# Gated window attention on one core: part of the output products, a gate and the sums of the last group rearranged

## The chip, the cores and the metric

The kernel runs on one core of a Trainium2 chip. The metric is the device time of one execution, in microseconds (us), taken as the median of the runs. All times below are in us unless ns is said.

## The reference

Eight batches of 1024 tokens with 512 features are normalised, sent through an attention with 16 heads of 32 features, multiplied by a gate, and added to the input. The mask repeats every 256 tokens: token i sees token j where i mod 256 is not below j mod 256.

```python
xn = _layernorm(x, axis=-1)
# attention, per head:
scores = jnp.einsum('bhid,bhjd->bhij', q, k) / jnp.sqrt(dk)
im = jnp.arange(L) % W                       # W = 256
scores = jnp.where(im[:, None] >= im[None, :], scores, NEG_INF)
attn = jnp.einsum('bhij,bhjd->bhid', softmax(scores), v)
s = jnp.einsum('bld,ed->ble', attn_as_rows, Wo) + bo
# gate:
w = (weights >= 0.0) * 2.0 - 1.0
g = _silu(jnp.clip(jnp.einsum('bsi,oi->bso', xn, w) * scale + bias, -100, 100))
x = x + s * g
```

q, k and v are products of xn with Wq, Wk and Wv plus their biases.

## The kernel before

A batch has 8 tiles of 128 tokens. Tokens are put in an order in which the mask is nearly triangular, so that much of the score matrix is never computed. The 16 heads are taken in four groups of four (NC = 4); a step of the program's main loop (line 1109) works on one group of one batch, and on one of nine *quads* (NQ = 9). A quad is a block of scores of four heads, 128 keys by 512 queries in all, and fills the one PSUM tile "quad" of four banks. There are 8 x 4 x 9 such steps.

In step n of group (b, g), `probs_quad` (586) computes the scores of the quad (the shift by the maximum, the mask and the product of keys and queries are matmuls into the same PSUM) and one exp of 128 x 2048 on ScalarE. The result goes into a tile "p" of two buffers, or, for quads 0 and 7, into the tile "total" of its half. `attend_quad` (633) multiplies the quad before with the values. Every group has two halves f of 512 queries: f = 1 has quads 0 to 6, f = 0 has quads 6 to 8 (quad 6 belongs to both). Beside this, `maxima_quad` (501) computes the same scores of the *next* group in the same PSUM tile and VectorE takes their maxima. The last group of all has no next one, and so no maxima.

The softmax's denominators: in all groups but the last, GpSimd adds the quads up in the tile "total" (`add_probs`, 649), and one product with ones per half sums over the keys (`sum_keys`, 678). In the last group `sum_quad` (693) sums every quad with its own product on TensorE. `keep_sum` (673) copies sums out of PSUM on ScalarE, `invert` (713) takes reciprocals on VectorE, one part of 128 queries at a time, and `normalise_heads` (717) multiplies with the attention of the half (PSUM tile "av", two buffers).

All other matmuls are `product`s (346): four chunks of four matmuls into one tile "bank" of PSUM (a pool of two), and an `after` that empties it. Such are queries and keys (`heads_work`), values (`values_work`), the plain gates, and the outputs (`output_work`, 726: product with Wo over the four groups, then on VectorE the bias bo is added and the gate multiplied, and GpSimd adds the residual). A gate (`gate_work`, 417) is either one in two passes of 8 fast matmuls ("G" in the plans) or a plain product of 16 matmuls ("H"). Its `after` scales and shifts on VectorE (both read the PSUM tile) and clamps on GpSimd; then `squash` (tanh on ScalarE), `finish` (VectorE) and a store to DRAM follow as pieces of work of their own. An output tile fetches its gate tile from there.

The order of the work is written out by hand. Each group has a plan, a string of words (lines 804 to 821): "q20" is half 0 of the queries of group 2, "V4" the values of tile 4, "O4" output tile 4 of the batch before, "G2" and "H2" the gate of tile 2, a ' means the next batch; words ahead of a bar may be run in the group before already. Squash and finish of a gate in the last batch are put three and four words behind it. `Beside.fill` (953) runs this work beside the steps: the costs of a group's words are spread evenly over its nine steps, and chunks are split to fit. [...]

The last group of batch 7 has the plan "-", no work of its own. After it come the eight output tiles of batch 7, in the order 4, 5, 6, 7, 0, 1, 2, 3, with tiles fetched two ahead; the inversion of each tile of half 0 is put one tile ahead (1207 to 1224). The last tile goes out in two halves, on SyncE's and ScalarE's queues (`last_output`, 750). Stores and fetches of all other tiles stand on SyncE's queue in program order.

Of the kernel before, what the change touches and what calls it, by code (L numbers as in the profile page):

```python
# [9 lines left out]
F32 = mybir.dt.float32  # L10
# [63 lines left out]
def tile_gated_window_attention(  # L74
# [554 lines left out]

    av = {}  # L630
    aT = {}

    def attend_quad(b, g, n):
        segs, _ = segments(n)
# [53 lines left out]
            )  # L688
        keep_sum(b, g, f, ps)

    sums = {}

    def sum_quad(b, g, n):

        segs, _ = segments(n)
        for k, (f, j, lo, w, at) in enumerate(segs):
            first = n == FIRST[f]
            last = n == LAST[f] and all(s[0] != f for s in segs[k + 1 :])
            if first:
                sums[f] = bank(f"sum_{b}_{g}_{f}")  # L700
            for h in range(NH):
                nc.tensor.matmul(  # L702
                    sums[f][head_rows(h), lo : lo + w],
                    lhsT=ones,
                    rhs=pts[b, g, n][:, h, at : at + w],
                    start=first,
                    stop=last,
                    skip_group_check=True,
                )
            if last:  # L710
                keep_sum(b, g, f, sums[f])

    def invert(b, g, f, part):
        r = aT[b, g, f][:, part * P : (part + 1) * P]
# [2 lines left out]
    def normalise_heads(b, g, f, part=None):  # L717
        cols = slice(0, HALF) if part is None else slice(part * P, (part + 1) * P)
        nc.vector.tensor_tensor(  # L719
            aT[b, g, f][:, cols], av[b, g, f][:, cols], aT[b, g, f][:, cols], ALU.mult  # L720
        )


    back = {}

    def output_work(b, it):
        def fetch():
            g = xres.tile([P, D], F32, tag="io", name=f"gb_{b}_{it}")
            nc.sync.dma_start(g, gd[b][it])

            where, tag = (xres, "io") if b + 1 < B else (xpool, "x")
            xr = where.tile([P, D], F32, tag=tag, name=f"xb_{b}_{it}")
            nc.sync.dma_start(xr, tokens(x, b, it))
            back[it] = g, xr

        def after(ps):
            gb, xr = back.pop(it)
            s = temp(f"s_{b}_{it}")
            nc.vector.tensor_tensor(ps, ps, rows["bo"], ALU.add)
            nc.vector.tensor_tensor(s, ps, gb, ALU.mult)  # L740
            nc.gpsimd.tensor_tensor(s, s, xr, ALU.add)  # L741
            nc.sync.dma_start(tokens(out, b, it), s)

        pairs = [
            (lambda g=g: (aT[b, g, it // 4][:, (it % 4) * P : (it % 4 + 1) * P], wT["wo"][:, g, :]))
            for g in range(NC)
        ]
        return fetch, product(f"o_ps_{b}_{it}", pairs, 0.86, after, lambda: it in back, True)

    def last_output(b, it):  # L750

        gb, xr = back.pop(it)
        s = temp(f"s_{b}_{it}")

        def ahead():
            nc.gpsimd.tensor_tensor(s, gb, rows["bo"], ALU.mult)
            nc.gpsimd.tensor_tensor(xr, xr, s, ALU.add)  # L757

        def rest():
            for part, queue in enumerate((nc.sync, nc.scalar)):  # L760
                at = slice(part * 256, part * 256 + 256)
                ps = bank(f"o_ps_{b}_{it}_{part}")
                for g in range(NC):
                    for h in range(NH):
                        cols = slice((it % 4) * P + h * DK, (it % 4) * P + (h + 1) * DK)
                        nc.tensor.matmul(
                            ps[head_rows(h), 0:256],
                            lhsT=aT[b, g, it // 4][:, cols],
                            rhs=wT["wo"][:, g, at],
                            start=(g == 0),  # L770
                            stop=(g == NC - 1),
                            skip_group_check=True,
                        )
                nc.vector.tensor_tensor(s[:, at], ps[:, 0:256], gb[:, at], ALU.mult)  # L774
                nc.vector.tensor_tensor(s[:, at], s[:, at], xr[:, at], ALU.add)  # L775
                queue.dma_start(tokens(out, b, it)[:, :, at], s[:, at])

        return ahead, rest

    def row_work():  # L780
# [20 lines left out]

    STEADY = (
# [10 lines left out]
    )  # L815
    CLOSING = (
# [4 lines left out]
    )  # L821

    class Block:
        def __init__(self, at, main):
# [17 lines left out]
    def plan(b, g, text):  # L842
        for word in text.split():
            kind, number = word[0], word.strip("'")[1:]
            bb = b + word.count("'")
            i = len(blocks)
            if kind == "|":
                for block in blocks:
                    block.early = block.early or block.at == (b, g)
                continue  # L850
            if kind == "N":
                half = int(number)
                stats, scale, normalise, turn = norm_work(b + 1, half)
                for k in range(4):
                    done = lambda key=(b + 1, 4 * half + k): key in normed
                    there = lambda key=(b + 1, 4 * half + k): key in xt
                    link(
                        i - 5 + (2 + k // 2 if half else 0) + k // 2,
                        Work(0, stats[k], late=True, ready=there),
                    )  # L860
                    by = lambda key=(b + 1, half): key in scaled
                    link(i + half + max(1, k), Work(0, normalise[k], ready=by))
                    link(i + half + 2 + k, Work(0.5, turn[k], turn=True, ready=done))
                link(i - 2 + 2 * half, Work(0, scale, late=True, ready=there))
                continue
            if kind == "-":
                main = []
            elif kind in "qk":
                main = heads_work(bb, int(number[0]), int(number[1]), kind)
            elif kind == "V":  # L870
                main = values_work(bb, int(number))
            elif kind == "W":
                main = [Work(0.5, turn_weight("wo")[int(number)], turn=True)]
            elif kind == "R":
                spread, main = row_work()
                link(i - 3, spread)
            elif kind == "O":
                fetch, main = output_work(b - 1, int(number))
                link(i - 1, fetch)
            else:  # L880
                split, main, squash, finish = gate_work(bb, int(number), kind == "H")
                if split is not None:
                    link(i - 3, split)
                later = 1 if b in (0, B - 1) else 0
                link(i + 2 + later, squash)
                link(i + 3 + later, finish)
            blocks.append(Block((b, g), main))

    for b in range(B):
        for g in range(NC):  # L890
            n0 = len(blocks)
            plan(b, g, (OPENING if b == 0 else STEADY if b + 1 < B else CLOSING)[g])
            if b + 1 == B:
                continue
            if g == 0:
                for it in range(4):
                    link(n0 + 1 + it, lambda b=b, it=it: load_x(b + 1, it))
            elif g == 1:
                for k in range(4):

                    ready = lambda key=(b + 1, k - 1): key[1] < 0 or key in turned
                    fn = lambda b=b, it=4 + k: load_x(b + 1, it)
                    link(n0 + 5 + k, Work(0, fn, ready=ready), True)
# [205 lines left out]
    for s, (b, g, n) in enumerate(steps):  # L1109
# [22 lines left out]
        probs_quad(b, g, n)  # L1132
        if s:
            attend_quad(*steps[s - 1])
            if last and n:
                sum_quad(*steps[s - 1])
            else:
                add_probs(*steps[s - 1], held=True)
        if add:
            sum_keys(*add)  # L1140
            invert(*add, 0)
# [14 lines left out]
        if nxt is not None:  # L1156
# [2 lines left out]
                shift_parts(1)  # L1159
            if n == 8:  # L1160
                shift_parts(0)
        if not last:

            add_probs(b, g, n)
        if add:
# [36 lines left out]

    b, g = B - 1, NC - 1
    attend_quad(b, g, NQ - 1)
    sum_quad(b, g, NQ - 1)
    units = {it: output_work(b, it) for it in range(NT)}
    order = (4, 5, 6, 7, 0, 1, 2, 3)
    for it in order[:2]:
        units[it][0]()
    for i, it in enumerate(order):  # L1210
        if i + 2 < NT:
            units[order[i + 2]][0]()
        if i + 1 < NT and order[i + 1] < 4:

            invert(b, g, 0, order[i + 1])
# [1 line left out]
        if it == order[-1]:  # L1217
            rest()
            continue
        if it == order[-2]:  # L1220
            ahead, rest = last_output(b, order[-1])
            ahead()
        for w in units[it][1]:
            w.run()
# [45 lines left out]
```

## Time and profile before

| | us |
|---|---|
| median of 3 runs | 2217.09 (2216.05 to 2217.92) |
| the profiled execution's own time | 2218.44 |
| its span | 2216.6 |
| last group, first scores to end of the last sum | 2148.63 to 2183.15 |
| eight output tiles and the last stores | 2183.15 to 2216.6 |

Sizes of operations (mean of one, ns): exp of 128x2048 on ScalarE 1878; reciprocal of 128x128 on VectorE 928; addition of 128x512 on GpSimd in `add_probs` 1284, for the residual 1369; VectorE operations of 128x512 with an operand in PSUM 691. The granted TensorE clock is 1.00 in the last group and 0.97 behind it. 256 KB fetches of the gate land after 2.9 (median), of the residual's input after 3.1, stores after 2.5; the two last stores of 128 KB after 2.3 and 2.9.

The busy times by stretch give, for each stretch of the span, its length and the busy time of each engine. In the timeline, each line is: start, length, engine, line of the program, operation, output and inputs, count, and in brackets the idle time of the engine before it with what ended it. In the chain of waits each line is a start, a length and the work or wait that the end of the program hung on.

### The profile page before, as it was taken

To read this page: it belongs to the slowest core of one execution; us is meant where nothing else is said; L and a number is where in the kernel's file an instruction comes from. 1 tells how busy PE (TensorE), PEld (TensorE's weight loads), DVE (VectorE), ACT (ScalarE), POOL (GpSimd) and SP (SyncE) were. 2 spreads that over 40 slices of the span, in tenths; PEclk is the share of its full clock that TensorE was granted. 3 is DMA by queue.
4 is the path that set the end of the run, shared out by engine and by line. 5 is a ranking of instruction groups with operands and counts; after the bars stand their busy time and mean duration, and the time that the engine had idled before them with its cause. 6 is when DMAs were issued, how large, how long until landed. Compare 5 with 4: busy or idle time off the path is not lost. (4 is left out here: it accounts for less than half of the span.)

```text
span 2216.6 us, 57362 instructions
## 1 busy us (share of the span) xinstructions
PE 2185.2 (99%) x26015; PEld 857.7 (39%) x26015; DVE 1276.9 (58%) x1635; ACT 875.2 (39%) x862; POOL 1325.5 (60%) x1198
## 2 busy tenths in 40 slices
PE   8999999999999999999999999999999999999998
PEld 4334333343333443333333333334333443333333
DVE  4556556665557655566555665565655665555564
ACT  2235433443444444344343443434443443343332
POOL 1256566656566656576557665556765666755662
PEclk9999999999999999999999999999999999999999
DMA  4001000121001210012000120002200111000113
GB/s 167 2 16 32 13 7 30 54 73 35 25 26 39 72 35 25 25 57 74 16 25 25 63 68 16 25 25 68 63 16 26 44 63 59 11 20 25 44 54 125
DMA packets 49676, 93.60 MB, mean 42 GB/s; under 512 B 5388, under 2 KB 5656, under 8 KB 49432
## 3 DMA queue, kind: packets, MB, share of 16 engines
q1 hardware_dynamic: 48728, 88.76, 12.2%
q8 instruction: 203, 3.33, 0.6%
q10 hardware_dynamic: 704, 1.18, 0.2%
q14 instruction: 41, 0.34, 0.0%
HBM read 56.37 MB, written 33.55 MB: 41 GB/s over the span
## 5 line engine op out<-in xcount | busy, mean ns | idle before, releaser
L659 POOL TENSOR_TENSOR p<-p,p 128x512 f32<-128x512 f32 x930 | 1096.3, 1209 | 394.2 <-ACT p L627 240.6
L537 DVE TENSOR_REDUCE pm<-s 128x4 f32<-128x2048 f32 (+3 forms) x384 | 663.8, 1749 | 589.9 <-PE s L525 588.1
L627 ACT ACTIVATE p<-t 128x2048 f32<-128x2048 f32 x288 | 540.8, 1878 | 843.9 <-PE t L614 769.4
L715 DVE RECIPROCAL aT<-aT 128x128 f32<-128x128 f32 x256 | 230.3, 928 | 217.6 <-ACT aT L676 217.6
L525 PE MATMUL s<-k,q 32*128 32x512 f32 (+3 forms) x3072 | 315.3, 504 | 1.6 <-ACT q L401 0.8
L640 PE MATMUL av<-p,v 128*32 128x512 f32 (+3 forms) x3072 | 308.2, 496 | 1.9 <-DVE aT L719 1.4
L614 PE MATMUL t<-q,k 32*128 32x512 f32 (+3 forms) x3072 | 306.7, 493 | 0.0
L358 PE MATMUL k_ps<-xnT,wkT 128*32 128x512 f32 (+3 forms) x2824 | 254.9, 478 | 1.7 <-ACT wkT L274 0.7
L358 PE MATMUL q_ps<-xnT,wqT 128*32 128x512 f32 (+2 forms) x2656 | 254.5, 497 | 2.0 <-ACT xnT L329 1.0
L358 PE MATMUL v_ps<-wvT,xnT 128*32 128x512 f32 (+3 forms) x2720 | 254.7, 490 | 0.0
L358 PE MATMUL o_ps<-woT,aT 128*32 128x512 f32 (+2 forms) x2584 | 244.1, 501 | 1.5 <-ACT shift L572 0.8
L741 POOL TENSOR_TENSOR s<-s,xb 128x512 f32<-128x512 f32 x63 | 86.2, 1369 | 216.5 <-DVE s L740 214.4
L614 PEld LDWEIGHTS t<-q,k 32*128 32x128 f32 x3072 | 139.1, 185 | 25.8
L358 PEld LDWEIGHTS k_ps<-xnT,wkT 128*32 128x32 f32 x2824 | 83.3, 109 | 168.9 <-issue 138.9
L640 PEld LDWEIGHTS av<-p,v 128*32 128x32 f32 x3072 | 70.5, 108 | 197.0 <-issue 164.4
L358 PEld LDWEIGHTS q_ps<-xnT,wqT 128*32 128x32 f32 x2656 | 78.7, 109 | 174.5 <-issue 151.8
L358 PEld LDWEIGHTS v_ps<-wvT,xnT 128*32 128x32 f32 x2720 | 78.9, 109 | 168.2 <-issue 143.5
L525 PEld LDWEIGHTS s<-k,q 32*128 32x128 f32 x3072 | 116.9, 184 | 53.5 <-ACT p L627 43.7
L456 PE MATMUL y_ps<-fwT,x 128*128 128x512 f32 x464 | 135.3, 418 | 1.7 <-ACT k L401 1.3
L358 PEld LDWEIGHTS o_ps<-woT,aT 128*32 128x32 f32 x2584 | 76.7, 110 | 152.8 <-issue 134.7
L429 POOL TENSOR_TENSOR x<-xnT,x 128x512 fp32r<-128x512 f32 x58 | 74.1, 1278 | 101.1 <-ACT x L428 101.1
L435 POOL TENSOR_SCALAR y<-y 128x512 f32<-128x512 f32 x64 | 39.6, 619 | 153.9 <-DVE y L434 111.8
(96 smaller groups left out, 1476.7 us busy)
## 6 DMA issues: line engine op xcount, KB each, us to landing
g<-t SPq DMA_DIRECT2D x64, 256.0 KB, 2.0
gb<-g SPq DMA_DIRECT2D x64, 256.0 KB, 2.9
xb<-in_L_attn_x_dram SPq DMA_DIRECT2D x64, 256.0 KB, 3.1
out_dram<-s SPq DMA_DIRECT2D x63, 256.0 KB, 2.5
x<-in_L_attn_x_dram SPq DMA_DIRECT2D x62, 256.0 KB, 3.1
wq_st<-in_L_attn_Wq_dram SPq DMA_DIRECT2D x2, 512.0 KB, 6.4
wv_st<-in_L_attn_Wv_dram SPq DMA_DIRECT2D x2, 512.0 KB
fw_st<-in_L_ffn_weights_dram SPq DMA_DIRECT2D x2, 512.0 KB, 9.4
```

What stands on the lines that cost most here:

```text
L358: nc.tensor.matmul(hold[0][cols, lo:hi], lhsT=lhsT[:, cols], rhs=rhs[:, lo:hi], start=(i == 0 and lo == 0), stop=(i == n - 1), skip_group_ ...
L429: nc.gpsimd.tensor_tensor(part[1], src, part[0].bitcast(F32), ALU.subtract)
L435: nc.gpsimd.tensor_scalar(y[0], y[0], MAX_VAL, -MAX_VAL, ALU.min, ALU.max)
L456: nc.tensor.matmul(hold[0], lhsT=part[i][:, c, :], rhs=wT["fw"][:, c, :], start=(i == 0 and c == 0), stop=(i == 1 and c == NC - 1),)
L525: nc.tensor.matmul(sc[:, h, at : at + w], lhsT=qt[b, g][head_rows(h), i * P : (i + 1) * P], rhs=kt[b, g][head_rows(h), lo:hi], start=(at = ...
L537: nc.vector.tensor_reduce(pm[:, 0 if lo == 0 else 1, i, :], sc[:, :, at : at + w], AX.X, ALU.max)
L614: nc.tensor.matmul(sc[:, h, at : at + w], lhsT=kt[b, g][head_rows(h), j * P : (j + 1) * P], rhs=qt[b, g][head_rows(h), q0 : q0 + w], start ...
L627: nc.scalar.activation(pt[:, :, :width], sc[:, :, :width], AF.Exp, scale=SCALE)
L640: nc.tensor.matmul(av[b, g, f][head_rows(h), lo : lo + w], lhsT=vt[b, j][:, g * P + h * DK : g * P + (h + 1) * DK], rhs=pts[b, g, n][:, h, ...
L659: nc.gpsimd.tensor_tensor(t[:, hs, lo : lo + w], t[:, hs, lo : lo + w], p[:, hs, at : at + w], ALU.add)
L715: nc.vector.reciprocal(r, r)
L741: nc.gpsimd.tensor_tensor(s, s, xr, ALU.add)
```

## The change

1. The last but one batch has a plan of its own for its last group, BEFORE_LAST, without G1'. The gate of tile 1 becomes the plain gate H1 in the last group.
2. In the last group, after H1, three of the four chunks (groups 0 to 2 of the heads) of output tiles 4, 5, 6, 0 and 1 are run beside the exps ("P4 P5 P6 P0 P1", `first_output`). Their `after` adds bo and keeps the partial sum in SBUF. They are ready once the half of group 2 that they read is normalised (`ended`).
3. GpSimd adds up quads 1 to 5 of half 1, and quad 6 of half 0, as in the other groups; `sum_last` makes one product over the total and one over the quad that is left. `sum_quad` goes.
4. Behind the last group the tiles go in the order 4, 7, 5, 2, 6, 3, 0, 1. Those begun have one chunk left, and add the partial sum where others add bo. Tiles are fetched three ahead, the gate tiles into the pool of the values. The last tile (now 1, begun) multiplies by the gate inside PSUM and adds the prepared residual from there; its preparation is issued ahead of tile 3, not of the last but one tile.

```diff
+    def sum_last(b, g, f, n):
+        ps = bank(f"sum_{b}_{g}_{f}")
+        own = [(lo, w, at) for f2, j, lo, w, at in segments(n)[0] if f2 == f]
+        parts_of = [(pts[b, g, TOTAL[f]], 0, HALF, 0)] + [(pts[b, g, n], *seg) for seg in own]
+        for k, (p, lo, w, at) in enumerate(parts_of):
             for h in range(NH):
                 nc.tensor.matmul(
+                    ps[head_rows(h), lo : lo + w],
                     lhsT=ones,
+                    rhs=p[:, h, at : at + w],
...
+        keep_sum(b, g, f, ps)
...
+    def first_output(b, it):
+        def after(ps):
+            n = len(begun)
+            if n % 2 == 0:
+                two[0] = qk.tile([P, L], F32, tag="qk"[n // 2 % 2], name=f"begun_{it}")
+            begun[it] = two[0][:, n % 2 * D : (n % 2 + 1) * D]
+            nc.vector.tensor_tensor(begun[it], ps, rows["bo"], ALU.add)
+        return product(
+            f"o_ps_{b}_{it}_begun", [(lambda g=g: output_pair(b, it, g)) for g in range(NC - 1)],
+            0.86, after, lambda: (b, NC - 2, it // 4) in ended, True,
+        )
...
-            g = xres.tile([P, D], F32, tag="io", name=f"gb_{b}_{it}")
+            where, tag = (xres, "io") if b + 1 < B else (vpool, "v")
+            g = where.tile([P, D], F32, tag=tag, name=f"gb_{b}_{it}")
...
-            nc.vector.tensor_tensor(ps, ps, rows["bo"], ALU.add)
+            nc.vector.tensor_tensor(ps, ps, rows["bo"] if row is None else row, ALU.add)
...
-                nc.vector.tensor_tensor(s[:, at], ps[:, 0:256], gb[:, at], ALU.mult)
-                nc.vector.tensor_tensor(s[:, at], s[:, at], xr[:, at], ALU.add)
+                nc.vector.tensor_tensor(ps[:, 0:256], ps[:, 0:256], gb[:, at], ALU.mult)
+                nc.vector.tensor_tensor(s[:, at], ps[:, 0:256], xr[:, at], ALU.add)
...
+    BEFORE_LAST = STEADY[:3] + ("k01' V1' | q11' G0' V2' k10' V3' k11' q10'",)
     CLOSING = (
         "V4 V5 | q20 V7 V6 k20 q21 k21",
         "O4 O5 | q30 k30 O6 q31 O7 k31",
         "H2 O0 H3 O1 H4 O2 H5 O3 H6 H7 |",
-        "-",
+        "H1 P4 P5 P6 P0 P1",
     )
...
-            if last and n:
-                sum_quad(*steps[s - 1])
-            else:
-                add_probs(*steps[s - 1], held=True)
+            add_probs(*steps[s - 1], held=True)
+            if last and n == LAST[1] + 1:
+                sum_last(b, g, 1, n - 1)
...
-        if not last:
+        if not last or n < LAST[1]:
             add_probs(b, g, n)
...
-    sum_quad(b, g, NQ - 1)
-    units = {it: output_work(b, it) for it in range(NT)}
-    order = (4, 5, 6, 7, 0, 1, 2, 3)
-    for it in order[:2]:
+    sum_last(b, g, 0, NQ - 1)
+    order = (4, 7, 5, 2, 6, 3, 0, 1)
+    units = {it: output_work(b, it, begun.get(it)) for it in range(NT)}
+    for it in order[:3]:
         units[it][0]()
     for i, it in enumerate(order):
-        if i + 2 < NT:
-            units[order[i + 2]][0]()
+        if i + 3 < NT:
+            units[order[i + 3]][0]()
...
-        if it == order[-2]:
-            ahead, rest = last_output(b, order[-1])
+        if it == order[-3]:
+            ahead, rest = last_output(b, order[-1], begun[order[-1]])
             ahead()
```

More of the change, by code (lines that the diff above doesn't have):

```diff
@@ L631, in tile_gated_window_attention @@
     aT = {}
+    ended = set()
     def attend_quad(b, g, n):
@@ L689, in sum_keys @@
         keep_sum(b, g, f, ps)
[L691 to L700, printed above, removed]
+    def sum_last(b, g, f, n):
[3 more added lines that the diff above has]
+        for k, (p, lo, w, at) in enumerate(parts_of):
             for h in range(NH):
                 nc.tensor.matmul(
-                    sums[f][head_rows(h), lo : lo + w],
+                    ps[head_rows(h), lo : lo + w],
                     lhsT=ones,
-                    rhs=pts[b, g, n][:, h, at : at + w],
-                    start=first,
-                    stop=last,
+                    rhs=p[:, h, at : at + w],
+                    start=(k == 0),
+                    stop=(k == len(own)),
                     skip_group_check=True,
                 )
-            if last:
-                keep_sum(b, g, f, sums[f])
+        keep_sum(b, g, f, ps)
     def invert(b, g, f, part):
@@ L721, in normalise_heads, with output_pair, output_work @@
         )
+        ended.add((b, g, f))
     back = {}
-    def output_work(b, it):
+    begun, two = {}, {}
+    def output_pair(b, it, g):
+        return (
+            aT[b, g, it // 4][:, (it % 4) * P : (it % 4 + 1) * P], wT["wo"][:, g, :]
+        )
[9 more added lines that the diff above has]
+            0.86, after, lambda: (b, NC - 2, it // 4) in ended, True,
+        )
+    def output_work(b, it, row=None):
         def fetch():
-            g = xres.tile([P, D], F32, tag="io", name=f"gb_{b}_{it}")
+            where, tag = (xres, "io") if b + 1 < B else (vpool, "v")
+            g = where.tile([P, D], F32, tag=tag, name=f"gb_{b}_{it}")
             nc.sync.dma_start(g, gd[b][it])
@@ L744, in output_work, with last_output @@
         pairs = [
-            (lambda g=g: (aT[b, g, it // 4][:, (it % 4) * P : (it % 4 + 1) * P], wT["wo"][:, g, :]))
-            for g in range(NC)
+            (lambda g=g: output_pair(b, it, g))
+            for g in range(0 if row is None else NC - 1, NC)
         ]
         return fetch, product(f"o_ps_{b}_{it}", pairs, 0.86, after, lambda: it in back, True)
-    def last_output(b, it):
+    def last_output(b, it, row):
         gb, xr = back.pop(it)
@@ L755, in ahead @@
         def ahead():
-            nc.gpsimd.tensor_tensor(s, gb, rows["bo"], ALU.mult)
+            nc.gpsimd.tensor_tensor(s, gb, row, ALU.mult)
             nc.gpsimd.tensor_tensor(xr, xr, s, ALU.add)
@@ L762, in rest @@
                 ps = bank(f"o_ps_{b}_{it}_{part}")
[L763 to L773, printed above, removed]
-                nc.vector.tensor_tensor(s[:, at], ps[:, 0:256], gb[:, at], ALU.mult)
-                nc.vector.tensor_tensor(s[:, at], s[:, at], xr[:, at], ALU.add)
+                lhsT, rhs = output_pair(b, it, NC - 1)
+                for h in range(NH):
+                    nc.tensor.matmul(
+                        ps[head_rows(h), 0:256], lhsT=lhsT[:, head_rows(h)], rhs=rhs[:, at],
+                        start=True, stop=True, skip_group_check=True,
+                    )
+                nc.vector.tensor_tensor(ps[:, 0:256], ps[:, 0:256], gb[:, at], ALU.mult)
+                nc.vector.tensor_tensor(s[:, at], ps[:, 0:256], xr[:, at], ALU.add)
                 queue.dma_start(tokens(out, b, it)[:, :, at], s[:, at])
@@ L819, in tile_gated_window_attention @@
         "H2 O0 H3 O1 H4 O2 H5 O3 H6 H7 |",
[1 row of a table removed]
[1 row of a table added]
     )
+    BEGUN = (4, 5, 6, 0, 1)
     class Block:
@@ L865, in plan @@
                 continue
-            if kind == "-":
-                main = []
-            elif kind in "qk":
+            if kind in "qk":
                 main = heads_work(bb, int(number[0]), int(number[1]), kind)
@@ L871, in plan @@
                 main = values_work(bb, int(number))
+            elif kind == "P":
+                main = first_output(bb, int(number))
             elif kind == "W":
@@ L887, in plan @@
             blocks.append(Block((b, g), main))
+    PLANS = [OPENING] + [STEADY] * (B - 3) + [BEFORE_LAST, CLOSING]
     for b in range(B):
@@ L891, in tile_gated_window_attention @@
             n0 = len(blocks)
-            plan(b, g, (OPENING if b == 0 else STEADY if b + 1 < B else CLOSING)[g])
+            plan(b, g, PLANS[b][g])
             if b + 1 == B:
@@ L1204, in tile_gated_window_attention @@
     attend_quad(b, g, NQ - 1)
-    sum_quad(b, g, NQ - 1)
-    units = {it: output_work(b, it) for it in range(NT)}
-    order = (4, 5, 6, 7, 0, 1, 2, 3)
-    for it in order[:2]:
+    sum_last(b, g, 0, NQ - 1)
+    order = (4, 7, 5, 2, 6, 3, 0, 1)
+    assert set(begun) == set(BEGUN)
+    units = {it: output_work(b, it, begun.get(it)) for it in range(NT)}
+    for it in order[:3]:
         units[it][0]()
     for i, it in enumerate(order):
-        if i + 2 < NT:
-            units[order[i + 2]][0]()
+        if i + 3 < NT:
+            units[order[i + 3]][0]()
         if i + 1 < NT and order[i + 1] < 4:
```

## The prediction

> **What bounds it now.** I read the page first, then the busy times by stretch (for the whole span and for the last two stages), then the chain that ended last, then TensorE, VectorE, GpSimd and SyncE in order of time for the last two groups.
>
> ```profile
> PE 2185.2 (99%) x26015; PEld 857.7 (39%) x26015; DVE 1276.9 (58%) x1635; ACT 875.2 (39%) x862; POOL 1325.5 (60%) x1198
> ...
> 2148.60:2183.20 34.60, 30.92 (x412) 12.49 (x416) 15.50 (x26) 19.47 (x14) 3.63 (x4) 1.00 0.21 70
> 2183.20:2216.60 33.40, 27.61 (x288) 9.19 (x280) 16.53 (x26) 0.58 (x1) 11.44 (x9) 0.97 0.43 143
> ```
>
> TensorE is busy 99% of the span. The second and third lines are the stages the change is about (length, then busy PE, weight loads, DVE, ACT, POOL): the last group, and the eight output tiles after it. GpSimd does 3.63 us of work in the first and is free.
>
> ```profile
> 2170.60 0.40 PE t L592 x8
> 2171.00 0.11 PE t L603 x8
> 2171.11 0.96 PE t L614 x16
> ...
> 2172.16 1.89 ACT p L627
> 2174.04 0.04 issue
> 2174.09 0.40 PE t L592 x4
> ...
> 2183.15 9.83 PE o_ps L358 x89
> ...
> 2203.87 3.58 DMA gb<-g
> ```
>
> In the last group the chain alternates: scores, exp (1.89), scores. There is one score quad in PSUM, so a step takes 3.33 to 3.49. Beside the exp PE does attention (0.88) and the sum (0.86); some 0.4 a step is lost. From 2183.15 eight products of 3.43 follow, and 33.45 pass to the end. Call the first scores of the group t(0), 2148.63, and the end of its last sum T0, 2183.15: 34.5 lie between.
>
> ```profile
> 2087.58 0.41 PE L566 MATMUL mT_ps<-identb,mt 128*32 128x128 bf16 x16 [0.26 <-DVE y L434]
> 2094.83 4.96 POOL L659 TENSOR_TENSOR p<-p,p 128x512 f32<-128x512 f32 x4
> 2099.82 0.61 POOL L435 TENSOR_SCALAR y<-y 128x512 f32<-128x512 f32 x1
> 2101.80 4.96 POOL L659 TENSOR_TENSOR p<-p,p 128x512 f32<-128x512 f32 x4 [1.37 <-ACT p L627]
> 2107.59 1.66 POOL L741 TENSOR_TENSOR s<-s,xb 128x512 f32<-128x512 f32 x1 [0.83 <-DVE s L740]
> 2123.18 5.23 POOL L659 TENSOR_TENSOR p<-p,p 128x384 f32<-128x384 f32 x5
> 2194.86 0.94 DVE L715 RECIPROCAL aT<-aT 128x128 f32<-128x128 f32 x1
> 2195.83 0.29 DVE L719 TENSOR_TENSOR aT<-av,aT 128x128 f32<-128x128 f32 x1
> 2196.95 0.70 DVE L739 TENSOR_TENSOR o_ps<-o_ps,bo_r 128x512 f32<-128x512 f32 x1 [0.83 <-PE o_ps L358]
> 2197.68 0.69 DVE L740 TENSOR_TENSOR s<-o_ps,gb 128x512 f32<-128x512 f32 x1
> ```
>
> These price what comes: adding one quad on GpSimd costs 4.96 (5.23 for the split one), the gate's clamp 0.61. The first line is a product that waits until a gate's bank is read: the two "bank" tiles are used in turn. Inverting and normalising one tile is 1.26 of VectorE, one output tile 1.42.
>
> **What the Trainium skill says.** "PSUM — Partial Sum Buffer", section "Engine vs sequencer instructions": the GpSimd queue is a strict FIFO. The trace agrees: clamps and quad additions stand in program order, and GpSimd waits 111.8 us in all for the gates' VectorE work. "SBUF — State Buffer", section "Who interferes with whom": a VectorE operation with both inputs in SBUF contends with GpSimd's reads, one with at most one does not. The trace agrees: the L741 addition that takes 1.66 meets the gate's last step (L442, both inputs in SBUF), undisturbed ones take 1.28; in the tail L775 takes 1.02 beside GpSimd and 0.42 alone. "Perfetto Trace Analysis", section "Optimization Strategy": stages with different bounds may gain by interleaving; here the first stage has little idle TensorE to give, as the next part shows.
>
> **Part 1, the gate.** Taking G1' out of the last but one batch saves 2.26 of PE (two halves of 1.13, 1928.96 and 1931.19). PE is busy 99.8% there, and steps fall from 7.35 to 7.1, which later groups run at 7.15: I take 2.3 less ahead of t(0). If the chain of scores, exp and maxima is in the way, 1.5. As H1 it is a plain product and costs 4 x 0.86 = 3.44 in the last group.
>
> **Part 2, the last group.** PE's work there: sums leave, nine of 0.86 = 7.74; sum_last brings 1.29 + 1.72; H1 3.44 and fifteen chunks 12.9 come. With scores 1.19 to 1.36 and attention 0.88 a step, PE alone needs 40.9, against 34.5 now. Then the waits, from t(0) = 0. H1's first half runs in step 0; attention(0) waits for VectorE's normalisation as now (2154.62, at 6.0). H1 ends at 8.6, VectorE's two steps at 10.05, the clamp at 10.7. The clamp is issued ahead of the additions of quad 1, so these wait for it, though exp(1) is done at 7.4. P4's first piece takes the bank that H1 had (the shift product took the other), so PE stands from 8.6 to 10.1. P5 and P1 stand 0.8 each behind the 0.7 addition of the product before.
>
> GpSimd then has quads 1 to 5: 4 x 4.96 + 5.23 = 25.1, from 10.7 to 35.8. Three L442 operations fall into it; at 1.66 - 1.28 each that is 1.1, so 36.9. The p tiles have two buffers, so exp(3) to exp(6) wait for additions 1 to 4 (15.7, 20.7, 25.6, 30.6): mostly within the other waits. PE reaches sum_last of the first half at 34.8 and stands until 36.9. So GpSimd sets the time. After it: sum 1.29, the last pieces with one bank wait 2.5, step 8 with 3.42, attention and last sum 2.6: 46.8, or 12.3 more than the 34.5 of now. Bounds: 41 (no wait) to 52 (see the slow rival). What it hides: the five additions of bo, VectorE being idle for more than half of the stage; the four first fetches, which SyncE reaches after H1's gate is stored, in step 5, and which have about 15 us.
>
> **Part 3, the tail.** PE has 5 x 0.86 + 3 x 3.44 = 14.6 left of 27.5. VectorE is next: seven tiles at 1.42, four at 1.26, and four halves of 0.43 = 16.7, in an order written out. From T0: product 7 ends at 4.3; VectorE serves it to 5.7, tile 2's inversion to 7.0, tile 5 to 8.4, waits 0.9 for product 2, then runs through to 20.4. Each product waits for its bank, none longer than VectorE. The adding of the residual from PSUM removes the 1.02 above. GpSimd comes behind: the last fetch (tile 1) is issued after tile 2's store at 12.0, gb at 12.6, and lands after 3.58 as now, at 16.2. The two preparing operations of the last tile wait for it and stand ahead of the additions of tiles 3 and 0 on GpSimd: done at 21.4. The store of tile 0 goes out then, and the first half of the last tile behind it on SyncE at 22.1. From the last issue (2212.62) to the end now are 4.0, with less in flight behind it I take 3.8: 25.9, against 33.45, 7.5 less. Bounds: 24.0 (DVE's end plus 3.6) to 27.5 (slower landings).
>
> **Sum.** -2.3 + 12.3 - 7.5 = +2.5. The profiled execution has 2216.6 in its span and 2218.44 as its own time; it would become 2219.1 and 2220.9. Its own time lies 1.35 above the median of the runs, so the median comes to 2217.1 + 2.5 = 2219.6. A kernel of this kind can be told from no change from about 0.2% on, 4.4 us: my forecast is "no change that can be told".
>
> **Rivals.** *PE stays the bound, faster.* If GpSimd starts at exp(1)'s end and keeps up, and banks cost nothing, the group needs 41 (+6.5), the tail 24.2 (-9.2), the gate -2.3: 5.0 less, 2212.1. For it: PE is the bound everywhere now, and PE work falls by 3.5 in all. Against: the clamp's place in a queue that keeps order.
>
> *GpSimd slows down, slower.* The place is the 21 additions of the last group. Now undisturbed ones take 1.24; the mean of all 128x512 ones is 1.284, and those that meet VectorE's SBUF work 1.66. At 1.5 each, 21 x 0.26 = 5.5 come on the path: 2225.1. Slower is decided from +1.9 on, at 1.33 each. For it: no slack, as every p tile waits for its addition. Against: most VectorE work here reads PSUM.
>
> *The change doesn't do what it says.* If readiness (the set of ended halves) holds the five products back, all 15 chunks run at the end of the group behind the GpSimd wait: some 7 us more than the forecast, 2227. Against: the halves of the group before are normalised in steps 0 and 4, before P4 and P0 are due.
>
> **Numbers.** Forecast 0.44, own range 2214 to 2221.4. PE bound 0.22, GpSimd slower 0.31, products held back 0.03. So faster 0.22, within 0.44, slower 0.34. The range runs from the first rival's time less 0.6 to the second's: 2211.5 to 2225.
>
> **What would show it.** Right: in the changed profile the group from t(0) to its last sum lasts 46 to 48; GpSimd adds without a gap for 25 us after a clamp; a wait of about 2 us of the sum for GpSimd; a wait of 1.5 of the second output product for the gate's VectorE step; VectorE nearly solid in the tail, 25 to 27 us long. Wrong: sums that find GpSimd done, a group of 42 or less, or t(0) earlier by less than 1.5.

## The result and the profile after

The changed kernel takes 2222.09 us (median of 12 runs, 2220.7 to 2222.77), the kernel before, measured beside it, 2216.63 (12 runs, 2215.35 to 2217.92). The ratio is 1.0023, with a 95% interval of 1.0016 to 1.0031: 5.1 us more, 3.5 to 6.9. That lies inside the whole range of the forecast (2211.5 to 2225), 0.7 beyond the narrower range of its likeliest case (2214 to 2221.4), and just beyond the 0.2% that was taken as "no change that can be told"; the change makes the kernel slightly slower.

The busy times by stretch of the changed kernel, for the last group and for the output tiles after it (length, then busy PE, weight loads, DVE, ACT, POOL, the granted clock, DMA share and GB/s):

```profile
2145.05:2192.92 47.87, 43.00 (x555) 16.99 (x558) 23.16 (x34) 20.10 (x15) 32.94 (x28) 1.00 0.20 67
2192.92:2218.90 25.98, 16.32 (x148) 4.53 (x140) 15.68 (x26) 0.59 (x1) 11.38 (x9) 0.86 0.47 163
```

Three numbers say what happened. The last group grew from 34.52 to 47.87, the tail shrank from 33.45 to 25.98. The last but one batch's last group and what follows up to t(0), counted from 1889.37 before and from 1887.40 after, shrank from 259.26 to 257.65. Together: -1.6 + 13.35 - 7.5 = +4.2. (Before, the border between group and tail is the end of the last sum; in all other kernels it is the start of the product behind it, which lies 0.2 earlier. Group and tail are good to 0.2; their sum isn't touched.) The spans (2216.6 and 2218.9) differ by less, because the profiled execution of before was already 1.97 later at the start of that stretch, of which 1.6 arose between 402 and 697 us in work that is the same in both; the 12 runs of the kernel before differ by up to 2.6. So traces are compared below from the first scores of the last group of the last but one batch on; this stretch lasts 327.23 before and 331.50 after.

TensorE is busy for 98% of the span, 99% before. The changed kernel's waits between 2145 and 2193 (who waits, for whom, total, how often, the longest):

```profile
ACT p L627 <- POOL p L660: 12.5, 4, 3.5
...
POOL p L660 <- PE av L641: 6.4, 1, 6.4
...
PE t L592 <- ACT p L627: 2.7, 3, 1.0
```

The chain reads backwards. TensorE's scores wait for exps, and those exps wait 12.5 us, not for scores but for GpSimd: each exp needs one of two p tiles, and a p tile is free only when its quad has been added. The timeline shows where GpSimd stood, first its own lines, then TensorE's:

```profile
2155.40 0.61 POOL L435 TENSOR_SCALAR y<-y 128x512 f32<-128x512 f32 x1 [6.11 <-DVE y L434]
2155.98 26.31 POOL L660 TENSOR_TENSOR p<-p,p 128x512 f32<-128x512 f32 x21
2188.65 2.51 POOL L660 TENSOR_TENSOR p<-p,p 128x512 f32<-128x512 f32 x2 [6.37 <-PE av L641]
```

```profile
2151.92 1.90 PE L358 MATMUL y_ps<-fwT,xnT 128*32 128x512 f32 x16
2153.64 0.61 PE L358 MATMUL o_ps_begun<-woT,aT 128*32 128x256 f32 x8
...
2168.32 0.40 PE L592 MATMUL t<-shift,neg 3*128 3x384 bf16 x8 [0.77 <-ACT p L627]
...
2182.34 1.50 PE L700 MATMUL sum<-p,ones 128*32 128x512 f32 x16 [0.89 <-POOL p L660]
```

GpSimd waits 6.11 for the gate's VectorE step (2155.40 less 2145.05 is 10.35 after t(0)), clamps, and then adds for 26.31 without a gap. The sum of half 1 finds it at work and waits 0.89. The tail's last lines, from GpSimd's and from SyncE's queue:

```profile
2209.30 1.26 POOL L778 TENSOR_TENSOR s<-gb,begun 128x512 f32<-128x512 f32 x1 [1.13 <-DMA gb<-g]
2210.64 1.27 POOL L779 TENSOR_TENSOR xb<-xb,s 128x512 f32<-128x512 f32 x1
2211.86 2.49 POOL L762 TENSOR_TENSOR s<-s,xb 128x512 f32<-128x512 f32 x2
```

```profile
2206.38 0.53 SPq L751 DMA_DIRECT2D gb<-g  x1
2208.19 6.72 SPq L763 DMA_DIRECT2D out_dram<-s  x3
2215.01 0.55 SPq L794 DMA_DIRECT2D out_dram<-s  x1
```

The last tile's preparation waits 1.13 for its gate tile and stands ahead of the two additions of L762; these end at 2214.35, together with VectorE's last operation (2214.36), and the last store of SyncE goes out behind them.

### The profile page after: what moved, and what is told of

It reads as the page before. It is cut to its first block, busy times and chain, and to the rows that moved or that the text cites. A ratio compares the mean times of both kernels' runs of the same rounds, so it can differ in the third digit from the quotient of the medians.

```text
span 2218.9 us, 57392 instructions
## 1 busy us (share of the span) xinstructions
PE 2182.3 (98%) x26015; PEld 857.1 (39%) x26015; DVE 1282.4 (58%) x1640; ACT 875.5 (39%) x861; POOL 1352.6 (61%) x1220
## 5 line engine op out<-in xcount | busy, mean ns | idle before, releaser
L660 POOL TENSOR_TENSOR p<-p,p 128x512 f32<-128x512 f32 x953 | 1124.8, 1210 | 401.8 <-ACT p L627 241.0
L358 PE MATMUL o_ps<-woT,aT 128*32 128x512 f32 (+3 forms) x2480 | 234.5, 499 | 2.4 <-DVE s L761 1.6
L762 POOL TENSOR_TENSOR s<-s,xb 128x512 f32<-128x512 f32 x63 | 86.2, 1369 | 180.5 <-DVE s L761 180.5
```

Source lines behind the costliest of these rows:

```text
L358: nc.tensor.matmul(hold[0][cols, lo:hi], lhsT=lhsT[:, cols], rhs=rhs[:, lo:hi], start=(i == 0 and lo == 0), stop=(i == n - 1), skip_group_ ...
L660: nc.gpsimd.tensor_tensor(t[:, hs, lo : lo + w], t[:, hs, lo : lo + w], p[:, hs, at : at + w], ALU.add)
```

## The experiments

The theory was that the place of the clamp and the length of GpSimd's chain set the end of the last group. The first rival: TensorE's added work sets it, and GpSimd's waits are only where that shows. The second: the products begun ahead are worth nothing, as the tail is VectorE's. All edits are to the changed kernel unless said otherwise. "Stretch" is the length defined above. The medians come from separate measurements; the kernel before, measured beside each, had 2216.59 for e1 to e4, 2217.11 for e5 to e8 and 2216.64 for e9 and e10, so differences between medians are good to about 0.5.

| kernel | median (runs) | ratio to before, 95% | last group | tail | stretch |
|---|---|---|---|---|---|
| before | 2216.63 (12) | 1 | 34.52 | 33.45 | 327.23 |
| changed | 2222.09 (12) | 1.0023 (1.0016 to 1.0031) | 47.87 | 25.98 | 331.50 |
| e1 clamp on VectorE | 2218.80 (13) | 1.0010 (1.0002 to 1.0018) | 44.70 | 26.95 | 329.30 |
| e2 gate back | 2219.48 (21) | 1.0011 (1.0004 to 1.0018) | 43.20 | 26.26 | 328.74 |
| e3 sums alone | 2223.55 (5) | 1.0032 (1.0019 to 1.0044) | 42.01 | 33.06 | 334.33 |
| e4 no products ahead | 2223.35 (6) | 1.0030 (1.0019 to 1.0042) | 41.89 | 32.63 | 333.80 |
| e5 one head on VectorE | 2217.84 (12) | 1.0005 (0.9997 to 1.0013) | 44.18 | 26.22 | 328.07 |
| e6 fetch four ahead | 2220.50 (17) | 1.0018 (1.0011 to 1.0025) | 47.88 | 25.30 | 330.83 |
| e7 is e1, e5, e6 | 2216.20 (13) | 0.9997 (0.9988 to 1.0005) | 43.72 | 25.11 | 326.48 |
| e8 is e7, reciprocals on ScalarE | 2215.85 (13) | 0.9995 (0.9987 to 1.0004) | 43.74 | 24.71 | 326.11 |
| e9 longer chain | 2223.88 (5) | 1.0034 (1.0021 to 1.0047) | 49.96 | 25.56 | 333.18 |
| e10 is e8's edits, gate back | 2215.79 (13) | 0.9997 (0.9989 to 1.0005) | 42.06 | 25.48 | 326.79 |

**e1, the clamp taken off GpSimd's queue.** Only H1's clamp, which is last ahead of the additions, moves to VectorE.

```diff
-            nc.gpsimd.tensor_scalar(y[0], y[0], MAX_VAL, -MAX_VAL, ALU.min, ALU.max)
+            clamper = nc.vector if (b, it) == (B - 1, 1) else nc.gpsimd
+            clamper.tensor_scalar(y[0], y[0], MAX_VAL, -MAX_VAL, ALU.min, ALU.max)
```

> The changed kernel with one edit: the clamp of the gate H1 is done by VectorE instead of GpSimd, so that it no longer stands ahead of GpSimd's additions. Theory (GpSimd's chain of additions, begun late behind the clamp, sets the end of the last group): the additions begin when exp(1) is done, 3.5 us earlier, and the waits of TensorE for exps and for the sum (0.77 + 0.91 + 1.01 + 0.89) go; 3.4 us faster than the changed kernel, about 2218.7. Rival (TensorE's added work and the VectorE tail set the time, GpSimd only fills gaps that would be there anyway): no change, 2222.

Measured: 3.3 less by the medians, and 3.2 less in the last group. GpSimd's timeline of e1:

```profile
2152.85 26.56 POOL L661 TENSOR_TENSOR p<-p,p 128x512 f32<-128x512 f32 x21 [3.26 <-ACT p L628]
...
2207.68 1.28 POOL L779 TENSOR_TENSOR s<-gb,begun 128x512 f32<-128x512 f32 x1 [2.38 <-DMA gb<-g]
```

The additions start 7.50 after t(0) (2145.35) instead of 10.93, and wait now for the exp of their own quad. Nearly all of those 3.43 is found again at the group's end; the row of additions itself takes 26.56 for 26.31. One operation of 0.61 in the wrong place of a queue costs 3.2 to 3.3. The tail takes 0.97 more: it starts earlier, but the last gate tile doesn't come earlier by as much, as the wait of 2.38 shows.

**e2, the gate back in its batch.** Part 1 undone: no H1, and the old plan for the batch before the last.

```diff
-        "H1 P4 P5 P6 P0 P1",
+        "P4 P5 P6 P0 P1",
...
-    PLANS = [OPENING] + [STEADY] * (B - 3) + [BEFORE_LAST, CLOSING]
+    PLANS = [OPENING] + [STEADY] * (B - 2) + [CLOSING]
```

> The changed kernel with the gate of tile 1 back in the last but one batch (G1'), no H1. Theory (GpSimd's chain): without H1's clamp the additions begin at exp(1), 6.6 after the first scores instead of 10.9; the group lasts about 42.7 instead of 47.9, the group's start comes 1.6 later: 2218.5. Rival (TensorE's work counts): 3.44 less in the last group, 1.6 to 2.3 more ahead of it, about 2220.5.

Measured: 2.6 less by the medians, 2.8 less in the stretch; between the two expectations. The 21 runs spread more widely (2217.66 to 2220.90) than those of the other edits, so the trace is the better guide here. So the gate's move, which saves 1.6 ahead of t(0), costs 4.7 in the last group. But GpSimd's and TensorE's timelines of e2 hold something that the theory didn't have:

```profile
2155.62 4.98 POOL L660 TENSOR_TENSOR p<-p,p 128x512 f32<-128x512 f32 x4 [2.95 <-PE av L641]
```

```profile
2151.76 0.40 PE L592 MATMUL t<-shift,neg 3*128 3x512 bf16 x4 [0.84 <-ACT p L627]
...
2154.43 1.07 PE L641 MATMUL av<-p,v 128*32 128x512 f32 x8 [1.41 <-DVE aT L716]
```

With the clamp gone the additions of quad 1 still don't start at their exp's end. They write into quad 0's p tile, which attention(0) reads; so they wait 2.95 for attention(0), which itself waits for VectorE's normalisation. The start is 7.18 after t(0) here (2148.44). The "total" isn't a tile of its own, and its first addition has a reader ahead of it.

**e3, the sums alone.** The kernel before, with only its last group's sums given to GpSimd (part 3).

```diff
...
-            if last and n:
-                sum_quad(*steps[s - 1])
-            else:
-                add_probs(*steps[s - 1], held=True)
+            add_probs(*steps[s - 1], held=True)
+            if last and n == LAST[1] + 1:
+                sum_last(b, g, 1, n - 1)
...
-        if not last:
+        if not last or n < LAST[1]:
...
```

> The kernel before with the sums alone moved: GpSimd adds up quads 1 to 5, one product over the total and one over the last quad on TensorE. Nothing else changed. Theory (GpSimd's chain of some 26 us is longer than the exps it runs beside): the sum of the first half waits until 32.5 after the first scores, and the group ends at about 40.2 instead of 34.5: 5.6 us slower than before, 2222.2. Rival (the additions hide beside the exps, TensorE has 4.7 us less to do): not over 1 us slower than before, 2217.5 or less.

Measured: 7.0 more than before, 7.1 in the stretch. TensorE has nine sums of 0.86 less and sum_last's 3.0 more to do than before, and the group still takes 42.01 against 34.52. The busy times of e3's last group, and its GpSimd and TensorE lines:

```profile
2146.93:2188.94 42.01, 32.38 (x354) 12.78 (x358) 17.37 (x26) 19.48 (x14) 31.74 (x27) 0.84 0.17 58
```

```profile
2154.91 25.71 POOL L659 TENSOR_TENSOR p<-p,p 128x512 f32<-128x512 f32 x21 [3.74 <-PE av L640]
```

```profile
2152.93 1.87 PE L640 MATMUL av<-p,v 128*32 128x512 f32 x8 [1.41 <-DVE aT L715]
...
2167.18 0.62 PE L592 MATMUL t<-shift,neg 3*128 3x384 bf16 x8 [2.60 <-ACT p L627]
```

Scores wait up to 2.60, and GpSimd adds without a gap: its chain sets this group. The rival of "TensorE's work" is refuted for it. One part is something else. TensorE is busy for 32.38 here and for 30.92 before, with less to do, because its granted clock in this group is 0.84 in the mean, against 1.00. Attention(0) took 1.87, against 1.06 before, so the additions, which wait for it, started 7.98 after t(0), 0.8 later than in e2 at full clock: some 0.8 of the 7.5 is the clock's, by this estimate. The slow stretch from 2167 to 2177 (0.51) costs nothing, as GpSimd adds through it. Why the clock fell isn't shown: the kernel before has the same wait of 1.41 ahead of attention(0) and keeps 1.00.

**e4, no product begun ahead.** As e2, with no P words; tiles keep the new order, the last tile again in four chunks.

```diff
...
-        "H1 P4 P5 P6 P0 P1",
+        "-",
...
-    BEGUN = (4, 5, 6, 0, 1)
+    BEGUN = ()
...
```

> The changed kernel without the begun products and without the moved gate: all eight output tiles run in full behind the last group, in the new order, with the new fetches; the last tile as in the kernel before. Beside the gate_back kernel it shows what the begun products bring. Theory: the group is bound by GpSimd in both, so the products ahead cost the group about 2.5 us (42.7 against 40.2) and save the tail 7.4 (26 against 33.4): about 2222.5 to 2223.5, 4 to 5 us slower than with them. Rival (products ahead push out the group by their whole 12.9 us of TensorE work, which the tail gives back in part): this kernel is the faster one, by 1 us or more.

Measured: 3.9 more than e2 by the medians, 5.1 more in the stretch. The last group is 1.3 shorter than e2's, the tail 6.4 longer. Begun products do help by 4 to 5; the second rival falls. In the group 12.9 of products cost only 1.3, since they lie in TensorE's waits for GpSimd. As in e3, the clock in e4's group is 0.84 (1.00 in e2), and its additions start 7.84 after t(0) for 7.18; without that the products would cost about 2.0, an estimate (1.3 and 0.66).

**e5, one head's additions on VectorE.** GpSimd's chain loses five of 21 additions.

```diff
-                nc.gpsimd.tensor_tensor(
+                own = (b, g) == (B - 1, NC - 1) and h == NH - 1
+                (nc.vector if own else nc.gpsimd).tensor_tensor(
```

> The changed kernel, in whose last group VectorE does one head's share of every quad's addition (one instruction in four) and GpSimd the other three. Theory (length of GpSimd's chain): it shrinks from 26.3 to about 22 us, though it begins as late as before behind the clamp; TensorE's waits for exps and for the sum go: 3.3 us faster than the changed kernel, about 2218.8. Rival (the two engines get in each other's way, or the chain is not what counts): at least 2221.5.

Measured: 4.2 less than the changed kernel. GpSimd's and TensorE's lines:

```profile
2156.91 22.19 POOL L661 TENSOR_TENSOR p<-p,p 128x512 f32<-128x512 f32 x16
```

```profile
2179.15 1.50 PE L701 MATMUL sum<-p,ones 128*32 128x512 f32 x16 [0.24 <-POOL p L661]
```

The chain is 4.1 shorter, though VectorE's added reads slow each GpSimd addition to 1.39 (22.19 / 16); the group is 3.7 shorter.

**e9, the chain made longer.** GpSimd adds quad 6's part of half 1 as well, and TensorE loses that product.

```diff
+        own = own if f == 0 else []
...
-        if not last or n < LAST[1]:
+        if not last or n <= LAST[1]:
```

> The changed kernel, in whose last group GpSimd adds quad 6 of half 1 too (two additions more), and TensorE's sum of that half is one product over the total. Theory (GpSimd's chain sets the end of the group): 2 x 1.25 more in the chain, and 0.43 less of TensorE behind it: 2.1 us slower than the changed kernel, 2224.2. Rival (the chain is cover): 0.4 faster or the same, 2222 at most.

Measured: 1.8 more than the changed kernel (1.7 in the stretch). GpSimd's line, and TensorE's:

```profile
2156.20 28.88 POOL L660 TENSOR_TENSOR p<-p,p 128x512 f32<-128x512 f32 x23
```

```profile
2183.91 1.05 PE L701 MATMUL sum<-p,ones 128*32 128x512 f32 x4 [2.24 <-POOL p L660]
```

TensorE has less to do and the kernel is slower. The group is 2.1 longer for 2.57 more of additions. Shorter chains help and longer ones hurt, at nearly their own length: the theory is shown from both sides.

**e6, tiles fetched four ahead.** For the tail.

```diff
-    for it in order[:3]:
+    for it in order[:4]:
...
-        if i + 3 < NT:
-            units[order[i + 3]][0]()
+        if i + 4 < NT:
+            units[order[i + 4]][0]()
```

> The changed kernel with output tiles fetched four ahead instead of three. Theory of the tail (last fetch, then GpSimd's two preparing operations, the additions of tiles 3 and 0 behind them, then the stores): GpSimd's first preparing operation no longer waits 1.1 us for the fetch, the last two additions end when VectorE hands tile 0 over (1.3 us after it), and the last store goes out 0.5 us earlier: 2221.5. Rival (VectorE's chain alone sets the end): no change, 2222.1.

Measured: the tail is 0.7 shorter (25.30), the group the same (47.88). GpSimd's timeline:

```profile
2208.43 1.28 POOL L778 TENSOR_TENSOR s<-gb,begun 128x512 f32<-128x512 f32 x1
```

The preparation waits for nothing now. The median fell by 1.6, more than the trace shows, so 0.7 is what can be put down to the edit.

**e7, the three together**, and **e8, with the last reciprocals on ScalarE** (logarithm, then exp of its negative, in place of four VectorE reciprocals of half 0). The edit of e8 beside e7's:

```diff
+        if (b, g, f) == (B - 1, NC - 1, 0):
+            nc.scalar.activation(aT[b, g, f], ps, AF.Ln)
+            nc.scalar.activation(aT[b, g, f], aT[b, g, f], AF.Exp, scale=-1.0)
+            return
...
-                invert(b, g, 0, order[i + 1])
```

> The changed kernel with three edits: clamp of H1 on VectorE, one head in four added by VectorE, tiles fetched four ahead. Theory: the clamp's edit gives 3.3, the 0.8 us that the sum still waited for GpSimd go, and the tail, whose last preparation waited 2.4 us for its fetch in the run with the clamp's edit, gives 1.5: 2216.5, level with the kernel before. Rival (the waits come back elsewhere, on VectorE): 2218.5.

> As the run with three edits, and the reciprocals of the last half (4 x 0.97 us of VectorE in the tail) are done by ScalarE as exp(-ln(x)) straight from PSUM. If VectorE's chain sets the tail, it ends about 1.5 us earlier (then TensorE with its two banks is next): 2215, faster than both kernels. If the tail hangs on fetches and stores, no change: 2216.5.

Measured: e7 is 5.9 below the changed kernel, and no wait of TensorE for GpSimd is left in it: TensorE is busy for 42.74 of the group's 43.72 and is the bound again. e8 is 0.35 below e7, less than the two medians can tell apart. VectorE's busy time in the tail falls from 15.67 in e7 to 11.86 in e8, the tail only by 0.4, for VectorE waits for products instead, as its timeline in e8 shows:

```profile
2204.48 0.70 DVE L766 TENSOR_TENSOR o_ps<-o_ps,bo_r 128x512 f32<-128x512 f32 x1 [2.12 <-PE o_ps L358]
```

**e10, e8's edits with the gate back in its batch.** It asks whether the gate's move is worth anything once the clamp is out of the way.

> The changed kernel with the gate back in the last but one batch (G1', no H1), one head in four added by VectorE, tiles fetched four ahead, reciprocals of the last half on ScalarE. Beside the run with the same edits and H1 (2215.85) it prices the gate's move once GpSimd is no longer the bound. If TensorE's work counts, 3.44 less in the group against 1.6 to 2.3 more ahead: 1.2 to 1.8 faster, 2214.3. If H1 only fills time in which TensorE waits at the group's start (1.4 for attention and 0.8 for the exp, as in the run with the gate back): the same or 0.7 slower, 2216.5.

Measured: 2215.79, as e8 (2215.85). The move saves 1.6 ahead of t(0). In the last group the gate's product then lies where TensorE would have waited anyway: without it, the waits of 0.84 and 1.41 for exp(0) and for VectorE's normalisation are there. In the traces e10 has 1.6 more ahead of t(0), 1.7 less in the group and 0.8 more in the tail, which wasn't followed; by the medians nothing is left either way.

Of all these, e7, e8 and e10 lie 0.8 to 1.3 below the kernel before as it was measured beside them, with intervals that include 1. None is shown to be faster. Sums kept on TensorE beside the begun products weren't tried: a sum over several steps holds one of two banks for the whole of them, and the gate and the begun products would have to share the other. What that costs is not shown, so this alternative to part 3 stays open.

## Why the prediction was right and wrong

The likeliest case said +2.5 and "no change that can be told"; +5.1 was measured, +4.2 in the stages of the trace; the 0.9 between the two shows in no stage of the traces and stays open. The mechanism was right: GpSimd's additions set the last group, late by the clamp, and the tail is mended by less than that. Only the size fell on the other side of 0.2%, by 1.05 in the last group and 0.7 in the gate's term.

**The gate, -2.3 forecast, -1.6 measured.** The group without G1' is 1.96 shorter (66.14 to 64.18), close to the 2.26 of its work. The three groups after it take 0.35 more (193.12 to 193.47), which the term didn't have; what in them lasts longer wasn't followed.

**The last group, +12.3 forecast, +13.35 measured (47.87 against 46.8).** The clamp let the additions start at 10.93, not 10.7, and they took 26.31, not 26.2. So the sum came at 37.29, not 36.9. The rest is behind it. Step 8 was priced like a mean step, 3.42; it takes 3.80, scores to attention. Before the change it took 3.76 (2177.45 to 2181.21), so the row to use stood in the trace. The last sum was priced with its attention at 2.6 and took 3.04. Part of it is a wait for the addition of quad 6 of half 0 (2188.65, 2.51), which writes the p tile that attention(7) reads, and which waits 6.37 for that; this is the same kind of wait that e2 shows for quad 1. The working followed who needs an addition's result, and not whose tile it overwrites.

**The waits for banks never came.** P4's first piece was to stand 1.5 for H1's bank. It follows H1 without a gap (2153.64), and P5 doesn't wait either; the only wait of this sort is 0.38 of P1, for a copy of the sum. So the two banks weren't taken strictly in turn: P4 didn't wait for H1's bank, which VectorE read until 2155.31, and P1 waited for the sum's bank, not for P0's, which VectorE read until 2184.92. In both places it was the one that came free first. The line from which the working took the turn showed a single wait. The error cost nothing, because GpSimd set the time: it moved TensorE's waiting to three waits of scores (0.77 to 1.01) that were not foreseen.

**The tail, -7.5 forecast, -7.5 measured.** The preparation began at 16.4 after T0 for 16.2, GpSimd's last addition ended at 21.4 for 21.4, the last store of SyncE went at 22.1 for 22.1. The first of these is luck in part: the last gate tile's fetch was issued at 13.5 (2206.38), not 12.6, and landed within 2.9, not 3.58. VectorE ended at 21.4, not 20.4; 0.44 of this is the last half product, which took 1.08 for the 0.64 of the one before it, at a granted clock of 0.50. It is hidden, as GpSimd ends at the same time.

**The rivals.** "TensorE stays the bound" is refuted: e3 and e9 have less work for it and are slower. Its number, though, can be read from e7: with the clamp and one head off GpSimd, a group of 43.72 and a tail of 25.11 remain, not 41 and 24.2, and the stretch is 0.75 shorter than before where that rival had 5.0. TensorE's own 42.74 of work in the group is more than the 40.9 of the working, and the working's own line could have told: 30.92 busy before, less 7.74 of sums, plus 3.01, 3.44 and 12.9, is 42.5. "GpSimd slows down" didn't happen: the chain took 26.31 where the forecast had 26.2 (25.1 and 1.1), and that rival decides from 1.9 more on. It names the measured side of 0.2%, but not for its reason. "Products held back" is refuted by the line of P4 in step 1. Of the signs that were named, the group of 46 to 48 and the gapless additions came; the sum waited 0.89, not about 2, the wait of the second product for the gate didn't come, and VectorE, called nearly solid in the tail, was busy for 15.68 of 25.98.

The Trainium skill's "PSUM — Partial Sum Buffer", section "Engine vs sequencer instructions", calls GpSimd's queue a strict FIFO; e1 puts a price on it, 3.2 for one clamp. "SBUF — State Buffer", section "Who interferes with whom", has VectorE and GpSimd contend where VectorE reads both inputs from SBUF (that one input does not contend, as the prediction has it, the page says only outside its two-port modes). The trace agrees, on both sides: the 21 additions took 1.2 more than their 25.1 undisturbed (1.1 was forecast), and L442, 0.68 at 2150.90 ahead of them, took 1.25 to 1.61 beside them. With two of them in the row (e2) the 21 additions took 25.95, 0.85 more. One of the three:

```profile
2173.14 1.61 DVE L442 SCALAR_TENSOR_TENSOR t<-t,y 128x512 f32<-128x512 f32 x1
```

VectorE's loss wasn't in the working; it lay in time in which VectorE had nothing else to do.

## What to carry to other kernels

Moving work from a full engine to an idle one is priced by the idle engine's chain and its first start, not by the busy times: 21 additions of 1.25 in a row, held back 3.4 by one clamp, made a group that needs 43 us of TensorE last 47.9. For every instruction that is moved onto a queue, look both at what is queued ahead of it and at who still reads the tile that it overwrites. Price the last step of a loop from its own row, not from the mean one.

## What the runs showed of the hardware

Where VectorE, with two inputs from SBUF, ran beside GpSimd's additions, both gave way: L442 went from 0.68 to as much as 1.61, three of them costing GpSimd 1.2 in all. With VectorE adding a head in the same way (e5) GpSimd's additions took 1.39 each over the whole row, against 1.25 (26.31 / 21) in the changed kernel, so e5 gains less than the five additions that it takes away would give at 1.25 (6.3): 4.1.

TensorE's granted clock fell in e3's last group to 0.54 for 2 us (2152.9 to 2154.9) and to 0.51 for 10 us (2167.0 to 2177.2), and in e4's to 0.58 and 0.50 in the same stretches; it is 1.00 in the last group of all kernels that begin products there, and of the kernel before.

Logarithm and exp on ScalarE cost two table loads in e8, each of 1.28 us. The first (2185.86) lies in time in which ScalarE waits; this is the second:

```profile
2190.12 1.28 ACT L681 ACT_TABLE_LOAD   x1
```

Each costs twice what its operation does (0.60 and 0.63).
